# Moving whole-array blocks, reciprocals and graph weights within the attention loop of a two-layer graph kernel

## The chip, the cores and the metric

The kernel runs on one core of a Trainium2 chip. The metric is the device time of one execution in microseconds (us). The core has five engines with an instruction queue each: TensorE (PE in the profile, PEld for its weight loads), VectorE (DVE), ScalarE (ACT), GpSimd (POOL) and SyncE (SP, which here only issues DMAs). All arithmetic is float32.

## The reference

Input x has 16 batches of 1024 nodes with 256 channels; adj is a 1024 x 1024 matrix shared by the batches. Layer 0, cut to what matters here:

```python
c_adj = mean(fea, axis=1)                          # fea: x transposed to (B, 256, 1024)
diff  = c_adj[:, None, :] - c_adj[:, :, None]
A     = abs(abs(sigmoid(diff) - 0.5) - 0.5) * 2    # then made symmetric
g     = relu(einsum('bcn,bnm->bcm', fea, adj * A) * para)
q     = heads of g;  k, v = heads of x @ kv_w      # 4 heads of 64
out   = softmax(q @ k.T * scale) @ v
x     = layernorm(x + out)
```

Layer 1 is a graph convolution with the normalised adj, two linear layers with batch norms over all batches, a residual and a layernorm.

## The kernel before, in words

Layer 0 is one software-pipelined loop, layer 1 a plain sequence after it. The change touches the loop of layer 0 alone.

**Attention.** The scores are computed transposed (keys on the partitions) and the softmax is taken without a maximum: p = exp(scores), outputs and denominators are summed, and the outputs are divided at the end. The unit is (batch b, head pair pr, query half qh, key block m): 128 keys by 512 queries for two heads. `scores` (L768) runs its matmuls on quarters of the array, four side by side, into a PSUM tile ps (two buffers), and ScalarE takes the exponential into p (L773, four buffers). `outputs` (L789) multiplies p by v, also on quarters, accumulating over eight key blocks in two PSUM tiles po, and VectorE sums p into acc (L796 for the first two key blocks, L798 for the others). Eight units are a *group*. At its end ScalarE and VectorE bring po to oT (L802, L803).

**After a group.** `normalise` multiplies acc by ones (den, L813, quarters of the array, two PSUM tiles of the pool ps_t), ScalarE and VectorE add the two halves to drow (L818, L819), and SyncE writes drow to DRAM (den<-drow, L821) and gathers it back transposed as dcol (L824). VectorE takes the reciprocal r_all (L827). `residual` transposes oT (poT, L834, whole array), VectorE multiplies by r_all (o, L838), GpSimd adds to x (L843). With a batch's last group comes the layernorm: statistics on VectorE (L586, L587), the root on GpSimd (L577, L579), scaling on VectorE (L590), and a write of x to DRAM (L846).

**Preparing the next batch.** `prologue(b)` returns three lists. `first`: transposes of x (pxT, L671); the first of them also runs `begin`, which sums the rows of x (csum, L657), writes the negated means to DRAM element by element (c<-ncol, L662) and reads them back broadcast to all partitions (crow, L664). `side`: the weights, one Abs (L679) and one Tanh (L684, followed by VectorE's product with adj, L685) for each of eight node blocks, 16 entries in all; their eight buffers wg are shared by all batches. `steps`: four values (pv, L727, copied by VectorE, L731) and four keys (pk, L714, copied by ScalarE, L718), then 16 parts of the graph product pg (L697), of which every four end in qT on VectorE (L703) and ScalarE (L706). The steps use the whole array. Values and keys need xT; every four graph parts need all eight weights.

**The order.** Two units make a *burst*, so a batch has 16 bursts, numbered u = 0 to 15 here, and a group four. Iteration j of the loop issues the scores of burst j, the normalise that is due (two bursts after a group's end), and then, at the bursts that the table FULL names, a *whole-array block*: a due residual, four steps, and from u = 9 on some transposes of x. The outputs issued in iteration j are those of burst j - 1 (`back`). At u = 5 the x of two batches on is loaded (L633), into a buffer that the layernormed x of an earlier batch must have left.

TensorE's instructions keep this written order (`manual_schedule` names PE alone). On the other engines the planner of the language orders the instructions by when it believes that they can run, so a place in the source does not fix a place in those queues. Each engine then runs its queue in order, waiting on semaphores. All poT, pg, pv, pk, pxT and den tiles rotate through the two buffers of ps_t, so each must wait until the tile two before it has been read. SyncE's DMA issues are a queue in order too.

Of the kernel before, what the change touches and what calls it, by code (L numbers as in the profile page):

```python
# [515 lines left out]
def fast_path(  # L516
# [19 lines left out]
    nc = tc.nc  # L536
# [19 lines left out]
    def tile_t(name):  # L556
        return ps_t.tile([P, HALF], F32, tag="t", name=name)
# [23 lines left out]
    def layernorm(t, name):  # L581
        st = small.tile([P, NCH, 6], F32, tag="ln_st", name=f"st_{name}")
        mv = small.tile([P, NCH, 2], F32, tag="ln_mv", name=f"mv_{name}")
        rstd = small.tile([P, NCH], F32, tag="ln_rs", name=f"rs_{name}")
        for n in range(NCH):
            nc.vector.bn_stats(st[:, n, :], t[:, n, :])  # L586
            nc.vector.bn_aggr(mv[:, n, :], st[:, n, :])  # L587
        rsqrt(rstd, mv[:, :, 1], EPS)
        for n in range(NCH):
            nc.vector.tensor_scalar(  # L590
                t[:, n, :], t[:, n, :], mv[:, n, 0:1], rstd[:, n : n + 1], ALU.subtract, ALU.mult
            )
# [20 lines left out]
    with (  # L613
# [14 lines left out]
        r_all = l0c.tile([P, B * H, 4, 2], F32, name="r_all")  # L628
        st = {}

        def load_x(b):
            t = xp.tile([P, NCH, C], F32, tag="x", name=f"x_{b}")
            nc.sync.dma_start(t, x[b].rearrange("(n p) c -> p n c", p=P))  # L633
            st[b] = {"x": t}
# [125 lines left out]
        def scores(i):  # L760
            b, pr, qh, m = units[i]
            qT, kT = st[b]["qT"], st[b]["kT"]
            ps = tile_s(f"ps_{i}")
            for kh in range(2):
                for hd in range(2):
                    r = slice(hd * D, (hd + 1) * D)
                    ks = slice(m * P + kh * D, m * P + (kh + 1) * D)
                    nc.tensor.matmul(  # L768
                        ps[kh * D : (kh + 1) * D, hd * HALF : (hd + 1) * HALF], kT[r, pr, ks],
                        qT[r, pr, qh * HALF : (qh + 1) * HALF], start=True, stop=True,  # L770
                    )
            p = pp.tile([P, N], F32, tag="p", name=f"p_{i}")
            nc.scalar.activation(p, ps, AF.Exp)  # L773
            A[i] = p

        def outputs(i):
            b, pr, qh, m = units[i]
            s, p = st[b], A.pop(i)
            if m == 0:
                G[b, pr, qh] = {  # L780
                    "po": [tile_o(f"po_{i}_{kh}") for kh in range(2)],
                    "acc": accp.tile([P, N], F32, tag="acc", name=f"acc_{i}"),
                }
            g = G[b, pr, qh]
            for hd in range(2):
                h = 2 * pr + hd
                for kh in range(2):
                    r = slice(kh * D, (kh + 1) * D)
                    nc.tensor.matmul(  # L789
                        g["po"][kh][hd * D : (hd + 1) * D, :], s["v"][r, m, h * D : (h + 1) * D],  # L790
                        p[r, hd * HALF : (hd + 1) * HALF], start=(m == 0), stop=(m == NCH - 1),
                    )
            if m == 0:
                g["p0"] = p
            elif m == 1:
                nc.vector.tensor_add(g["acc"], g.pop("p0"), p)  # L796
            else:
                nc.vector.tensor_add(g["acc"], g["acc"], p)  # L798
            if m == NCH - 1:
                k = (b * PAIRS + pr) * 2 + qh  # L800
                g["oT"] = op.tile([P, HALF], F32, tag="oT", name=f"oT_{k}")
                nc.scalar.copy(g["oT"], g["po"][0])  # L802
                nc.vector.tensor_add(g["oT"], g["po"][1], g["oT"])  # L803

        def normalise(b, pr, qh):

            g = G[b, pr, qh]
            k = (b * PAIRS + pr) * 2 + qh
            den = [tile_t(f"den_{k}_{kh}") for kh in range(2)]
            for hd in range(2):  # L810
                for kh in range(2):
                    r = slice(kh * D, (kh + 1) * D)
                    nc.tensor.matmul(  # L813
                        den[kh][hd * D : (hd + 1) * D, :], ones[r, :],
                        g["acc"][r, hd * HALF : (hd + 1) * HALF], start=True, stop=True,
                    )
            row = rdp.tile([P, HALF], F32, tag="drow", name=f"drow_{k}")
            nc.scalar.copy(row, den[0])  # L818
            nc.vector.tensor_add(row, den[1], row)  # L819
            for hd in range(2):  # L820
                nc.sync.dma_start(den_d[k][hd : hd + 1, :], row[hd * D : hd * D + 1, :])  # L821
            col = small.tile([P, 4, 2], F32, tag="dcol", name=f"dcol_{k}")
            for hd in range(2):
                nc.sync.dma_start(  # L824
                    col[:, :, hd], den_d[k][hd : hd + 1, :].rearrange("o (n p) -> p (o n)", p=P)
                )
            nc.vector.reciprocal(r_all[:, k], col)  # L827

        def residual(b, pr, qh):
            g, s = G.pop((b, pr, qh)), st[b]  # L830
            k = (b * PAIRS + pr) * 2 + qh
            pt = tile_t(f"poT_{k}")
            for j in range(4):
                nc.tensor.transpose(  # L834
                    pt[:, j * P : (j + 1) * P], g["oT"][:, j * P : (j + 1) * P], ident
                )
            o = rdp.tile([P, 4, 2, D], F32, tag="o", name=f"o_{k}")
            nc.vector.tensor_mul(  # L838
                o, pt.rearrange("p (n h d) -> p n h d", h=2, d=D),
                r_all[:, k].unsqueeze(3).to_broadcast([P, 4, 2, D]),  # L840
            )
            xs = s["x"][:, 4 * qh : 4 * qh + 4, pr * P : (pr + 1) * P]
            nc.gpsimd.tensor_tensor(xs, xs, o.rearrange("p n h d -> p n (h d)"), ALU.add)  # L843
            if pr == PAIRS - 1 and qh == 1:
                layernorm(s["x"], f"l0_{b}")
                nc.gpsimd.dma_start(x1_d[b], s["x"])  # L846
                del st[b]

        def run(fs, k):
            for f, a in fs[:k]:  # L850
                f(*a)
            del fs[:k]
# [1 line left out]

        FULL = {1: 4, 4: 4, 6: 4, 9: 4, 11: 4, 14: 4}
        BURST = 2
        bursts = [range(i, i + BURST) for i in range(0, len(units), BURST)]
        PERB = PER // BURST  # L860
        with tc.manual_schedule(engines={mybir.EngineType.PE}):
            load_x(1)
            first, steps, side = prologue(0)
            run(first, 4)
            while steps:
                run(side, 4)
                run(steps, 2)
            next_first, next_steps, next_side = prologue(1)
            run(next_first, 4)
            full, quarter = {}, {}  # L870

            def back(j):

                for i in bursts[j]:
                    outputs(i)
                b, pr, qh, m = units[bursts[j][-1]]
                if m == NCH - 1:
                    quarter.setdefault(j + 2, []).append((normalise, (b, pr, qh)))
                    k = j + 4
                    while k % PERB not in FULL:  # L880
                        k += 1
                    full.setdefault(k, []).append((residual, (b, pr, qh)))

            for j in range(len(bursts)):
                b, u = j // PERB, j % PERB
                for i in bursts[j]:
                    scores(i)
                run(quarter.get(j, []), 9)
                if u == 0:
                    steps, side = next_steps, next_side  # L890
                    next_first, next_steps, next_side = [], [], []
                if u == 5 and b + 2 < B:
                    load_x(b + 2)
                    next_first, next_steps, next_side = prologue(b + 2)
                run(side, 3)
                if u in FULL:
                    run(full.get(j, []), 9)
                    run(steps, FULL[u])
                    if u >= 9:
                        run(next_first, 1 if u < 12 else 2)  # L900
                if j:
                    back(j - 1)
            j = len(bursts)
            back(j - 1)
            for k in range(j, j + 8):
                run(quarter.get(k, []), 9)
                run(full.get(k, []), 9)
# [278 lines left out]
```

## Time and profile before

The median of three runs is 3185.31 us (3184.79 to 3187.74); the profiled execution has a span of 3179.2 us.

| engine | busy us | share of the span |
|---|---|---|
| TensorE, matmuls | 2776.8 | 87% |
| TensorE, weight loads | 1213.2 | 38% |
| VectorE | 1416.8 | 45% |
| ScalarE | 1139.3 | 36% |
| GpSimd | 213.8 | 7% |

| group (one line, one engine) | count | busy us | mean ns |
|---|---|---|---|
| scores L768, TensorE | 4096 | 522.5 | 621 |
| outputs L789, TensorE | 4096 | 502.5 | 603 |
| graph product L697, TensorE | 1024 | 466.0 | 609 |
| exponentials L773, ScalarE | 512 | 499.1 | 1021 |
| accumulation L798, VectorE | 384 | 469.5 | 1223 |
| Abs L679 and Tanh L684, ScalarE | 256 | 271.2 | 1136 and 1043 |
| reciprocal L827, VectorE | 64 | 12.8 | 200 |

Matmuls are pipelined, so the mean of one is its latency, and busy us is the time in which at least one ran. The attention loop lasts until about 2070 us of the span; layer 1 follows. In the lines further down, the time in brackets is how long the engine stood idle before that instruction, and the name behind the arrow is what it was waiting for.

### The profile page before, as it was taken

Reading aid. Unit: us, or ns where it says so; the run is one execution under the profiler, and the core shown is the slowest. Engines: PE = TensorE matmul, PEld = TensorE weight load, DVE = VectorE, ACT = ScalarE, POOL = GpSimd, SP = SyncE. Lnnn points to the kernel's source line nnn. Section 1 sums busy time; section 2 is a strip of 40 time slices with the busy share of each in tenths; the row PEclk is TensorE's granted clock in tenths of the full one; section 3 lists DMA queues with packets and bytes.
Section 4 is the critical chain, followed back from the end, with each engine's and each line's share of the span. In section 5 each row is a group of like instructions: output and inputs, shape, how many; then the busy total and the mean of one; then the engine's idle time right before and its main releaser. Section 6 shows DMA issues by size and latency. Waiting matters only on the chain. (4 is left out here: it accounts for less than half of the span.)

```text
span 3179.2 us, 32796 instructions
## 1 busy us (share of the span) xinstructions
PE 2776.8 (87%) x13522; PEld 1213.2 (38%) x13522; DVE 1416.8 (45%) x2130; ACT 1139.3 (36%) x1313; POOL 213.8 (7%) x196
## 2 busy tenths in 40 slices
PE   6998898988988989889898899889999999999943
PEld 3433333333333333333333333364444444444432
DVE  3554554654545545455465454641111111233365
ACT  3454352552534535434255253400011111133284
POOL 0000001000000001000100000100000000000032
PEclk9999999998999999999999999969999999999955
DMA  4000101101011010010100101102212221144255
GB/s 126 8 19 16 34 1 34 28 7 34 1 34 33 2 34 15 20 34 1 34 28 8 34 1 38 31 27 93 96 76 80 79 80 66 53 172 159 106 185 199
DMA packets 122062, 169.00 MB, mean 53 GB/s; under 512 B 86704, under 2 KB 103600, under 8 KB 111664
## 3 DMA queue, kind: packets, MB, share of 16 engines
q1 hardware_dynamic: 112720, 99.70, 10.4%
q0 software_dynamic: 9184, 67.12, 5.3%
q8 instruction: 108, 1.77, 0.3%
q14 instruction: 50, 0.41, 0.0%
HBM read 99.36 MB, written 67.44 MB: 52 GB/s over the span
## 5 line engine op out<-in xcount | busy, mean ns | idle before, releaser
L768 PE MATMUL ps<-qT,kT 64*64 64x512 f32 x4096 | 522.5, 621 | 148.7 <-ACT p L773 148.7
L773 ACT ACTIVATE p<-ps 128x1024 f32<-128x1024 f32 x512 | 499.1, 1021 | 291.3 <-PE ps L768 290.6
L798 DVE TENSOR_TENSOR acc<-acc,p 128x1024 f32<-128x1024 f32 x384 | 469.5, 1223 | 251.7 <-ACT p L773 235.2
L789 PE MATMUL po<-p,v 64*64 64x512 f32 x4096 | 502.5, 603 | 4.9 <-DVE oT L803 4.9
L697 PE MATMUL pg<-wg,x 128*128 128x512 f32 x1024 | 466.0, 609 | 20.7 <-DVE drow L819 17.1
L998 PE MATMUL pagg<-ahT,x1l 128*128 128x512 f32 x1024 | 444.0, 593 | 0.0
L768 PEld LDWEIGHTS ps<-qT,kT 64*64 64x64 f32 x4096 | 155.5, 138 | 461.1 <-issue 233.3
L1017 ACT ACTIVATE hw<-ph,col_b 128x1024 f32<-128x1024 f32 x64 | 71.3, 1114 | 651.3 <-PE ph L1013 651.3
L697 PEld LDWEIGHTS pg<-wg,x 128*128 128x128 f32 x1024 | 193.8, 194 | 272.8 <-issue 247.4
L998 PEld LDWEIGHTS pagg<-ahT,x1l 128*128 128x128 f32 x1024 | 194.2, 190 | 241.1 <-issue 241.1
L789 PEld LDWEIGHTS po<-p,v 64*64 64x64 f32 x4096 | 152.0, 136 | 296.7 <-issue 286.1
L843 POOL TENSOR_TENSOR x<-x,o 128x512 f32<-128x512 f32 x64 | 109.0, 1704 | 1833.7 <-DVE o L838 1833.7
L706 ACT ACTIVATE qT<-qT 128x512 f32<-128x512 f32 x64 | 40.1, 626 | 532.5 <-DVE qT L703 532.5
L1077 PE MATMUL po<-hl,w2T 128*128 128x512 f32 x512 | 222.4, 597 | 6.9 <-ACT hl L1068 6.9
L1013 PE MATMUL ph<-agg,w1T 128*128 128x512 f32 x512 | 222.2, 592 | 0.0
L1002 DVE COPY agg<-pagg 128x1024 f32<-128x1024 f32 x32 | 39.2, 1224 | 377.8 <-PE pagg L998 377.8
L727 PE MATMUL pv<-kvw_s,xT 128*128 128x256 f32 x512 | 147.7, 439 | 57.5 <-DVE v L731 28.9
L685 DVE SCALAR_TENSOR_TENSOR wg<-wg,adj_s 128x1024 f32<-128x1024 f32 x128 | 153.3, 1219 | 36.7 <-ACT wg L684 36.7
L1019 DVE BATCH_NORM_STATS2 bn_st<-hw 128x6 f32<-128x512 f32 x128 | 82.3, 685 | 152.4 <-ACT hw L1017 152.4
L1077 PEld LDWEIGHTS po<-hl,w2T 128*128 128x128 f32 x512 | 98.1, 192 | 131.1 <-issue 122.4
L727 PEld LDWEIGHTS pv<-kvw_s,xT 128*128 128x128 f32 x512 | 108.5, 220 | 100.8 <-DVE v L731 42.1
L1013 PEld LDWEIGHTS ph<-agg,w1T 128*128 128x128 f32 x512 | 97.3, 190 | 122.5 <-issue 122.5
(87 smaller groups left out, 2011.4 us busy)
## 6 DMA issues: line engine op xcount, KB each, us to landing
h<-hw POOLq DMA_DIRECT2D x16, 2048.0 KB, 6.5
hl<-h SPq DMA_DIRECT2D x16, 2048.0 KB
x<-in_x_dram SPq DMA_DIRECT2D x16, 1024.0 KB
x<-x POOLq DMA_DIRECT2D x16, 1024.0 KB, 4.2
x1l<-x SPq DMA_DIRECT2D x16, 1024.0 KB
xf<-x SPq DMA_DIRECT2D x16, 1024.0 KB
out_dram<-xf POOLq DMA_DIRECT2D x16, 1024.0 KB, 5.2
crow<-c SPq DMA_DIRECT2D x16, 512.0 KB
```

Of the source, the lines that this page charges most:

```text
L685: nc.vector.scalar_tensor_tensor(w, w, 1.0, adj_s[:, n, :], op0=ALU.subtract, op1=ALU.mult)
L697: nc.tensor.matmul(ps, xt[:, n, c * P : (c + 1) * P], s["wg", n][:, hs], start=(n == 0), stop=(n == NCH - 1),)
L727: nc.tensor.matmul(pt[:, j * C : (j + 1) * C], s["xT"][:, c, n * P : (n + 1) * P], kvw_s[:, c, C : 2 * C], start=(c == 0), stop=(c == CC - 1),
L768: nc.tensor.matmul(ps[kh * D : (kh + 1) * D, hd * HALF : (hd + 1) * HALF], kT[r, pr, ks], qT[r, pr, qh * HALF : (qh + 1) * HALF], start=Tr ...
L773: nc.scalar.activation(p, ps, AF.Exp)
L789: nc.tensor.matmul(g["po"][kh][hd * D : (hd + 1) * D, :], s["v"][r, m, h * D : (h + 1) * D], p[r, hd * HALF : (hd + 1) * HALF], start=(m = ...
L798: nc.vector.tensor_add(g["acc"], g["acc"], p)
L843: nc.gpsimd.tensor_tensor(xs, xs, o.rearrange("p n h d -> p n (h d)"), ALU.add)
L998: nc.tensor.matmul(ps[:, hs], xt[:, m, c * P : (c + 1) * P], ahT[:, m, hs], start=(m == 0), stop=(m == NCH - 1),)
L1013: nc.tensor.matmul(ps[:, hs], w1T[:, c, k * P : (k + 1) * P], t[:, c, hs], start=(c == 0), stop=(c == CC - 1),)
L1019: nc.vector.bn_stats(bn1_st[:, k, 2 * b + half, :], ht[:, k, half * HALF : (half + 1) * HALF])
L1077: nc.tensor.matmul(ps[:, hs], w2T[:, k, c * P : (c + 1) * P], ht[:, k, hs], start=(k == 0), stop=(k == HC - 1),)
```

## The change

Four things are done together.

- The table FULL moves the six whole-array blocks from bursts 1, 4, 6, 9, 11, 14 to bursts 0, 4, 6, 8, 10, 12, and within an iteration the outputs (`back`) are now issued ahead of the block. At bursts 0, 4, 8 and 12 those outputs end a group, so the block stands between a group's last outputs and the next group's work, while oT is brought out of PSUM. The transposes of x move to bursts 10 and 12.
- The reciprocal is issued in `residual`, where its result is used, in place of `normalise`, where its operand has just been asked for from DRAM.
- A residual falls due five bursts after its group's last burst in place of four.
- The 16 entries of the weights are issued over ten bursts: two each at bursts 13, 14 and 15 of the batch before, and the other ten at bursts 0 to 5, one where a block stands and two elsewhere. Before, they were issued three at a time from burst 0 on. For batch 1 the first six are issued ahead of the loop.

```diff
         def normalise(b, pr, qh):
...
-            nc.vector.reciprocal(r_all[:, k], col)
+            g["col"] = col
 
         def residual(b, pr, qh):
             g, s = G.pop((b, pr, qh)), st[b]
             k = (b * PAIRS + pr) * 2 + qh
+            nc.vector.reciprocal(r_all[:, k], g["col"])
...
-        FULL = {1: 4, 4: 4, 6: 4, 9: 4, 11: 4, 14: 4}
+        FULL = {0: 4, 4: 4, 6: 4, 8: 4, 10: 4, 12: 4}
...
             run(next_first, 4)
+            run(next_side, 6)
...
-                    k = j + 4
+                    k = j + 5
                     while k % PERB not in FULL:
                         k += 1
...
-                run(side, 3)
+                if j:
+                    back(j - 1)
                 if u in FULL:
                     run(full.get(j, []), 9)
                     run(steps, FULL[u])
-                    if u >= 9:
-                        run(next_first, 1 if u < 12 else 2)
-                if j:
-                    back(j - 1)
+                    if u >= 10:
+                        run(next_first, 2)
+                if u > 12:
+                    run(next_side, 2)
+                else:
+                    run(side, 1 if u in FULL else 2)
```

## The prediction

> **What bounds the kernel now.** I read the page first, then who waits for whom on TensorE between 179 and 2029 us (the attention part), then the engines in order of time through one batch.
>
> ```profile
> PE 2776.8 (87%) x13522; PEld 1213.2 (38%) x13522; DVE 1416.8 (45%) x2130; ACT 1139.3 (36%) x1313; POOL 213.8 (7%) x196
> ...
> PE   6998898988988989889898899889999999999943
> ...
> PEclk9999999998999999999999999969999999999955
> ```
> TensorE is the bound. It is nearly full in the graph convolution (slices 27 to 37), but loses a tenth to a fifth in the attention slices, and those are what the change touches. Nothing after about 2070 us should move.
>
> ```profile
> PE ps L768 <- ACT p L773: 146.6, 51, 10.2
> PE pv L727 <- DVE v L731: 25.4, 14, 1.8
> PE poT L834 <- ACT drow L818: 24.2, 29, 0.8
> PE pv L727 <- DVE drow L819: 19.7, 14, 1.8
> PE pg L697 <- DVE drow L819: 16.0, 14, 1.1
> ```
> Columns: us in all, times, longest. So 60 us (24.2 + 19.7 + 16.0) come from whole-array blocks that start right after a denominator (den) and find both ps_t buffers taken. The large item, ps behind the exponentials p, is in time order on TensorE:
>
> ```profile
> 763.55 1.90 PE L789 MATMUL po<-p,v 64*64 64x512 f32 x16
> 775.68 3.69 PE L768 MATMUL ps<-qT,kT 64*64 64x512 f32 x16 [10.23 <-ACT p L773]
> 779.14 3.01 PE L789 MATMUL po<-p,v 64*64 64x512 f32 x16
> ...
> 785.56 0.66 PE L834 MATMUL poT<-ident,oT 128*128 128x128 f32 x4 [0.83 <-ACT drow L818]
> 787.35 8.83 PE L697 MATMUL pg<-wg,x 128*128 128x512 f32 x16 [1.14 <-DVE drow L819]
> ```
> TensorE stands 10.23 us at burst 8, then runs its next 16 matmuls in 3.69 instead of 1.90 us. The cause is on VectorE, ScalarE and the DMA queue:
>
> ```profile
> 758.23 2.29 DVE L657 TENSOR_REDUCE csum<-x 128x8 f32<-128x2048 f32 x1 [6.63 <-DMA x<-in_x_dram]
> 760.43 0.68 DVE L819 TENSOR_TENSOR drow<-den,drow 128x512 f32<-128x512 f32 x1
> ...
> 773.29 0.20 DVE L827 RECIPROCAL r_all<-dcol 128x8 f32<-128x8 f32 x1 [9.57 <-DMA dcol<-den]
> 773.41 0.64 DVE L703 SCALAR_TENSOR_TENSOR qT<-pg,para_s 128x512 f32<-128x512 f32 x1
> ```
> ```profile
> 774.08 0.63 ACT L706 ACTIVATE qT<-qT 128x512 f32<-128x512 f32 x1 [19.86 <-DVE qT L703]
> ```
> ```profile
> 753.02 0.37 SPq L633 DMA_DIRECT2D x<-in_x_dram  x1
> 761.14 0.54 SPq L821 DMA_DIRECT2D den<-drow  x2
> 761.77 0.38 SPq L662 DMA_DIRECT2D c<-ncol  x1
> 762.29 1.03 SPq L824 DMA_DIRECT2D dcol<-den  x2
> ```
> The row sum csum holds VectorE until x has landed, drow queues behind it, the gather dcol is issued behind the scattered write c, and the reciprocal waits 9.57 us. Behind it stands qT, behind that ScalarE's qT, then the exponentials of burst 7, then TensorE.
>
> **What the Trainium skill says.** "TensorE: Matmul & The Clock Gate", section "Architectural detail", has ScalarE and VectorE as strict FIFOs; the 19.86 us of ScalarE agree. The same page, "What's actually happening", has TensorE's clock halved after about 3.4 us of idleness; 3.69 against 1.90 us agree. "DMA: Bandwidth & Descriptors", "Rules for kernel authors", makes a strided last dimension one descriptor per element, and "Queues, rings and completion order" has each ring taken in order. Here c (4 KB) needs 10.5 us until crow, which waits for it, is issued (772.28), and dcol behind it needs 11.0 (762.29 to 773.29); at burst 9, without c, dcol lands 2.7 us after its issue (788.48 to the reciprocal at 791.21). Agreed.
>
> **One batch in numbers.** Burst 8 comes round every 129.7 us (256.47 to 1812.59 in 12 steps). Idle TensorE per batch: burst 8, mean 8.3 (13 stalls of 6.0 to 10.2); den before a block at bursts 1 and 9, 4.1; values at burst 4, 1.8; weights at burst 15, 2.8 (1.83 + 0.77 + 0.2); pxT, 0.35; 17.4 in all. Undisturbed work: 16 bursts x 3.43 (726.86 to 730.29), 6 blocks of about 7.1, den 4 x 0.87, transposes 8 x 0.5: 105.7. The remaining 6.6 us per batch is half clock.
>
> **Part by part.** I take the instruction order of the changed program as built, since only TensorE's order is written by hand, and lay the durations above along it.
>
> *Reciprocals.* Written later, but the planner still puts each on VectorE one accumulation after its drow, as it can run as soon as dcol is there. So this line alone buys little. What does change at burst 5: drow now stands ahead of csum, and dcol ahead of c on the queue. From the end of the GpSimd residual addition P (burst 4): layernorm ends P+7.1 (739.2 to 746.3); x is there 11.9 later (746.3 to 758.23), P+19.0; csum, ccol, ncol to P+21.6; accumulation, reciprocal, accumulation, qT: P+24.8 if dcol has landed; ScalarE's qT and one exponential: P+26.5; scores P+26.7. TensorE would be ready at P+24.4 (values resume P+2.2; second half of block 3.5; then S, den, O, S, O, graph block, S, O, with 0.4 lost at den). Stall 2.3 instead of 8.3. Dcol: its den write queues behind the load of x (issued P+13.8), so it lands between P+18 (2.7 after issue) and about P+22; the reciprocal's turn is P+22.8. Bounds: 1 if x comes sooner, 6 if the load or c slows dcol. I take 2.3: 6.0 x 13 = **78 us saved**.
>
> *Blocks at 0, 4, 6, 8, 10, 12.* None shares a burst with a den (1, 5, 9, 13) now: the 4.1 us go, in all 26.5 + 19.7 + 17.1 = **63 us saved**. No matmul is added. The evacuation oT that blocks behind group ends would hide cost TensorE only one wait of 4.9 in the whole trace: nothing. New small waits: values at burst 0 behind two batch-norm statistics, 0.5; burst 4, 0.2 more, as an accumulation goes ahead of o; den at burst 5 on the v copy behind the layernorm, 0.4; a second pxT wait at burst 10, 0.35; den at 13 behind xT, 0.3. 1.75 x 15 = **26 us lost**.
>
> *Weights over ten bursts.* As built they are not spread: the weight buffers come free with the last graph block (burst 12 now), and ScalarE gets all 16 Abs and Tanh after oT there, before the exponentials of burst 14, with only burst 13's two, one qT and one drow among them. In before, at burst 15, 14 such instructions took 13.5 us (690.60 to 704.09), 0.96 each; the 20 here take 19.2, from 0.7 after the block's start, plus the exponential: scores of burst 15 may go 21 us after the block's start. TensorE has until then: block 6.9, two pxT with their wait 1.8, S 1.7, den with wait 1.2, O, S, O 5.2: 16.8. Stall 4.3 instead of 2.8: 1.5 x 15 = **22 us lost**. Bounds 3.5 to 6.
>
> *Half clock.* No row shows it for this order. Bounds: none, or 7 per batch as now. After a 6 us stall, scores and outputs lost 1.8 + 1.1; the 1.82 us wait for values lost nothing (1.99 for the next part). I take about 2.9 for burst 15's stall and 0.9 for the rest: 3.8 against 6.6, 2.8 x 13 = **36 us saved**.
>
> Sum: 78 + 63 - 26 - 22 + 36 = 129; 3185 - 129 = **3056 us**.
>
> **Rivals.**
> (a) The stall at burst 8 stays. For it: the reciprocal is still early on VectorE, csum still waits for x, and den now queues behind the load. Against: dcol no longer follows c. Then the 78 and the half clock go: 63 - 26 - 22 = 15, about 3170 us; with dcol a little slower yet, 3150 to 3185.
> (b) Slower: as (a), and the clump of weights stalls 7 or more with its own half clock (another 3 + 3 per batch, 90 us): about 3250. For it: the clump is now contiguous before burst 14. Against: the count above gives 4.3.
> (c) Faster yet: short waits leave the clock whole and dcol arrives early; half clock near zero (50 more) and burst 8 at 1 us (17 more): about 2990.
>
> **How the numbers follow.** Forecast 0.72, (a) 0.12, (b) 0.05, (c) 0.11. The forecast's own spread: half clock 0 to 7 gives -50 to +42, burst 8 from 1 to 6 gives -17 to +48, burst 15 -12 to +25; together about 3005 to 3120. Leaving half of (c), all of (b) and most of (a) outside gives 3005 to 3125. Faster 0.93 (part of (a) is near no change), same 0.02, slower 0.05.
>
> **What would show it.** The wait of ps for p should fall from 147 to about 90 us, in two groups: near 2.3 at burst 8 and near 4.3 at burst 15. Waits of poT, pv and pg for drow should vanish. VectorE's wait for dcol, 204.5 us in all, should fall by more than half, and csum's wait for x stay near 6 to 8 each. The period of a batch should be near 120 us. I am wrong if the reciprocal still waits about 10 us at burst 6, if the load of x shifts, or if the weights stall TensorE more than 6 us.

## The result, and the profile after

The changed kernel takes 2991.39 us (median of 4 runs, 2989.65 to 2992.18) against 3186.52 us for the kernel before on the same chip. The ratio is 0.9381, with a 95% interval of 0.9362 to 0.9401. So it is faster, by more than forecast: 3056 us was forecast, and the time lies 14 us below the range. The profiled execution has a span of 2990.3 us.

The page of the changed kernel, first TensorE's busy time, then its busy tenths and its granted clock in 40 slices:

```profile
PE 2736.4 (92%) x13522; PEld 1202.2 (40%) x13522; DVE 1418.0 (47%) x2130; ACT 1138.6 (38%) x1313; POOL 185.7 (6%) x196
...
PE   6999999999999999999999999799999999999842
...
PEclk9999999999999999999999999699999999999955
```

The number of instructions is the same on every engine, and the busy time of VectorE and ScalarE has not moved by more than 1.2 us. All attention slices of TensorE between the first and the last now show a 9 where 8 and 9 alternated: the gain is mostly waiting time that went. GpSimd is busy 28 us less, which matters further down.

TensorE's waits in the attention part of the changed kernel (179 to 1900 us): us in all, times, longest.

```profile
PE ps L768 <- ACT p L773: 69.6, 20, 4.5
PE pv L727 <- DVE v L731: 12.7, 14, 0.9
PE pxT L671 <- DVE qT L703: 9.0, 26, 0.3
```

The scores' wait for exponentials fell from 146.6 to 69.6 us, values' wait for their copies from 25.4 to 12.7, and the three waits for drow are gone. The 26 waits for pxT are the 0.35 at bursts 10 and 12, two in most batches.

One batch of the changed kernel in order of time, all engines, around burst 8 (burst 4 at the top, SPq is the DMA queue):

```profile
571.22 1.99 PE L727 MATMUL pv<-kvw_s,xT 128*128 128x256 f32 x8 [0.91 <-DVE v L731]
...
580.66 0.37 SPq L633 DMA_DIRECT2D x<-in_x_dram  x1
...
586.09 0.93 SPq L824 DMA_DIRECT2D dcol<-den  x2
586.15 2.29 DVE L657 TENSOR_REDUCE csum<-x 128x8 f32<-128x2048 f32 x1 [5.92 <-DMA x<-in_x_dram]
...
588.75 0.36 SPq L662 DMA_DIRECT2D c<-ncol  x1
...
589.76 0.20 DVE L832 RECIPROCAL r_all<-dcol 128x8 f32<-128x8 f32 x1
...
591.09 0.68 DVE L703 SCALAR_TENSOR_TENSOR qT<-pg,para_s 128x512 f32<-128x512 f32 x1
...
593.42 1.98 PE L768 MATMUL ps<-qT,kT 64*64 64x512 f32 x16
```

The gather dcol is now issued 2.66 us ahead of the scattered write c. The reciprocal, before which VectorE stood idle for 9.57 us in the batch shown of before, has no bracket: it starts without a wait that the view shows. The scores of burst 8, which followed a hole of 10.23 us, have none either.

What is left is at burst 15. TensorE of the changed kernel, and then ScalarE:

```profile
649.25 3.69 PE L768 MATMUL ps<-qT,kT 64*64 64x512 f32 x16 [4.46 <-ACT p L773]
652.72 2.54 PE L789 MATMUL po<-p,v 64*64 64x512 f32 x16
```
```profile
644.22 2.18 ACT L679 ACTIVATE wg<-crow,ccol 128x1024 f32<-128x1024 f32 x2
646.30 2.00 ACT L684 ACTIVATE wg<-wg 128x1024 f32<-128x1024 f32 x2
648.19 1.92 ACT L773 ACTIVATE p<-ps 128x1024 f32<-128x1024 f32 x2
```

The exponentials of burst 14 stand behind the last of 16 Abs and Tanh, which follow each other from 629.48 on with only the two exponentials of burst 13, one qT and one drow among them. The two groups of matmuls behind the hole take 3.69 and 2.54 instead of 1.90 us.

A batch now takes 115.5 us (burst 15 from 300.93 to 1686.67 in 12 steps) instead of 129.7.

### The profile page after: what moved, and what is told of

Its sections match the earlier page's. It is cut to its first block, busy times and chain, and to the rows that moved or that the text cites. A ratio compares the mean times of both kernels' runs of the same rounds, so it can differ in the third digit from the quotient of the medians.

```text
span 2990.3 us, 32734 instructions
## 1 busy us (share of the span) xinstructions
PE 2736.4 (92%) x13522; PEld 1202.2 (40%) x13522; DVE 1418.0 (47%) x2130; ACT 1138.6 (38%) x1313; POOL 185.7 (6%) x196
## 5 line engine op out<-in xcount | busy, mean ns | idle before, releaser
L768 PE MATMUL ps<-qT,kT 64*64 64x512 f32 x4096 | 519.1, 619 | 69.6 <-ACT p L773 69.6
L697 PE MATMUL pg<-wg,x 128*128 128x512 f32 x1024 | 454.4, 597 | 4.3 <-ACT kT L718 4.3
L789 PEld LDWEIGHTS po<-p,v 64*64 64x64 f32 x4096 | 166.3, 137 | 292.8 <-issue 289.6
L844 POOL TENSOR_TENSOR x<-x,o 128x512 f32<-128x512 f32 x64 | 81.1, 1267 | 1670.3 <-DVE o L839 1670.3
L727 PE MATMUL pv<-kvw_s,xT 128*128 128x256 f32 x512 | 128.0, 394 | 26.8 <-DVE v L731 16.1
L679 ACT ACTIVATE wg<-crow,ccol 128x1024 f32<-128x1024 f32 x128 | 140.8, 1137 | 17.2 <-PE pg L697 11.9
```

The source lines that it names most:

```text
L679: nc.scalar.activation(w, s["crow"], AF.Abs, bias=s["ccol"][:, n : n + 1])
L697: nc.tensor.matmul(ps, xt[:, n, c * P : (c + 1) * P], s["wg", n][:, hs], start=(n == 0), stop=(n == NCH - 1),)
L727: nc.tensor.matmul(pt[:, j * C : (j + 1) * C], s["xT"][:, c, n * P : (n + 1) * P], kvw_s[:, c, C : 2 * C], start=(c == 0), stop=(c == CC - 1),
L768: nc.tensor.matmul(ps[kh * D : (kh + 1) * D, hd * HALF : (hd + 1) * HALF], kT[r, pr, ks], qT[r, pr, qh * HALF : (qh + 1) * HALF], start=Tr ...
L789: nc.tensor.matmul(g["po"][kh][hd * D : (hd + 1) * D, :], s["v"][r, m, h * D : (h + 1) * D], p[r, hd * HALF : (hd + 1) * HALF], start=(m = ...
```

## The experiments

Ratios are against the kernel before on the same chip; three chips were used. The kernel before took 3185.2 us on that of the first four experiments below, 3208.83 on that of the means on another queue and of the first three experiments with an order written by hand, and 3188.2 on that of the other three. So ratios are compared, not times.

**Reciprocal alone.** The kernel before, with the one line moved.

```diff
-            nc.vector.reciprocal(r_all[:, k], col)
+            g["col"] = col
 ...
 def residual(b, pr, qh):
+            nc.vector.reciprocal(r_all[:, k], g["col"])
```

> The kernel before with one part of the change: the reciprocal issued in residual. As built, the instruction order of VectorE, ScalarE and the DMA queue is that of before, line for line. Theory A (the order that the planner gives decides, the place in the source does not): no change, 3180 to 3190 us, burst 8 still stalls 6 to 10 us. Rival B (the reciprocal's place frees VectorE): 3050 to 3110 us, burst 8 stalls under 3 us.

Measured: 3186.98 us, ratio 1.0006 (0.9994 to 1.0018). The waits are those of before (ps for p 146.8). The planner orders VectorE here, and moving this line in the source did nothing.

**Blocks alone.** The changed kernel, with the reciprocal and the weights issued as before.

```diff
...
-            run(next_side, 6)
...
-                if u > 12:
-                    run(next_side, 2)
-                else:
-                    run(side, 1 if u in FULL else 2)
+                run(side, 3)
```

> The changed kernel with the reciprocal back in normalise and the weights issued three a burst as before; what is left is the table of blocks, the outputs ahead of the block, and the residual's fifth burst. Theory A: the whole gain is here, 2985 to 3000 us. Rival B: the reciprocal and the weights carry a good part of it, 3040 us or more.

Measured: 2992.84 us, ratio 0.9389 (0.937 to 0.9407). The whole gain is in the table, the outputs ahead of the block and the residual's fifth burst. Spreading the weights in the source gained nothing: in the changed kernel all 16 still stand together behind burst 12's block.

**Outputs ahead of the block alone.** The kernel before with its old table.

```diff
+                if j:
+                    back(j - 1)
                 if u in FULL:
...
-                if j:
-                    back(j - 1)
```

> The kernel before with only the outputs issued ahead of the whole-array block; its table 1, 4, 6, 9, 11, 14 stays. As built, drow then stands ahead of csum on VectorE and dcol ahead of c on the queue. Theory A: burst 8 falls from 8.3 us to 0 to 2.5 (13 times), den has outputs of 1.7 us between it and the block, so the waits for drow fall from 60 us to under 10, and ScalarE's clump of weights now stalls TensorE about 4.5 us a batch: near 3000 us, 2980 to 3040. Rival C (the table's positions are what counts): 3110 us or more.

Measured: 2979.18 us, ratio 0.9347 (0.9328 to 0.9366): this alone gives all of it, and a little more than the whole change. The waits of this kernel on TensorE:

```profile
PE ps L768 <- ACT p L773: 61.1, 35, 3.1
PE pv L727 <- DVE v L731: 12.8, 14, 0.9
...
PE pv L727 <- DVE drow L819: 5.2, 12, 0.9
```

The hole at burst 8 falls to 0.6 us in the mean, in 5 of 13 batches. With the outputs ahead, drow has 1.7 us of matmuls more to be computed in, so even blocks that share a burst with a denominator hardly wait: of the 60 us of drow waits, 5.2 are left before pv and 4.4 before pg, without a new table. The holes in front of the scores that the weights leave are 0.56 and 3.11 us per batch, together 3.7 in place of 4.46.

**The table alone.** The changed kernel with the outputs behind the block again, except at u = 0.

```diff
-                if j:
+                if j and u == 0:
                     back(j - 1)
                 if u in FULL:
...
+                if j and u:
+                    back(j - 1)
```

> The changed kernel with the outputs back behind the block (except at burst 0, where values would overwrite a v still in use). As built, csum stands ahead of drow and c ahead of dcol again, as in before. Theory A: the waits for drow go (4.1 us a batch), burst 8 stalls 6 to 10 us as before, the clump of weights 4 to 5: 3110 to 3170 us. Rival C: 3000 to 3040 us.

Measured: 3091.46 us, ratio 0.9703 (0.9682 to 0.9724), better than expected. The drow waits are gone, but the hole at burst 8 stays (8.3 us in the mean). Burst 15, where the expectation put 4 to 5 us, has a hole of only 1.52 here; waits for oT of 14 us in all, which the whole change does not have, take back a part. DMA queue of this kernel, then TensorE:

```profile
729.95 0.53 SPq L821 DMA_DIRECT2D den<-drow  x2
730.58 0.38 SPq L662 DMA_DIRECT2D c<-ncol  x1
731.09 1.04 SPq L824 DMA_DIRECT2D dcol<-den  x2
```
```profile
732.11 1.90 PE L789 MATMUL po<-p,v 64*64 64x512 f32 x16
743.98 3.69 PE L768 MATMUL ps<-qT,kT 64*64 64x512 f32 x16 [9.97 <-ACT p L773]
```

Here csum still stands ahead of drow and c ahead of dcol. So it is the outputs ahead of the block that turn both orders round.

**The means on another queue.** Is it the queue that makes dcol late, or the DMA engines? The kernel before, with c and crow issued by GpSimd.

```diff
-                nc.sync.dma_start(c_d[b].rearrange("o (n p) -> p (o n)", p=P), ncol)
+                nc.gpsimd.dma_start(c_d[b].rearrange("o (n p) -> p (o n)", p=P), ncol)
...
-                nc.sync.dma_start(s["crow"], c_d[b][0].partition_broadcast(P))
+                nc.gpsimd.dma_start(s["crow"], c_d[b][0].partition_broadcast(P))
```

> The kernel before with the means' write c and read crow issued by GpSimd, so that dcol no longer stands behind c in SyncE's queue; csum still stands ahead of drow on VectorE. Theory A (c ahead of dcol is what makes the reciprocal late): dcol lands about 2.7 us after its issue, the stall at burst 8 falls from 8.3 to about 2.3 us in 13 batches with its half clock: 3070 to 3110 us. Rival D (what counts is csum ahead of drow, or the 16 DMA engines are shared so that c delays dcol from any queue): burst 8 stalls 5 us or more, 3140 us or more.

Measured: 3195.63 us, ratio 0.996 (0.9946 to 0.9974), so next to nothing; the hole at burst 8 has a mean of 8.7 us. SyncE's queue of this kernel, then GpSimd's, then VectorE:

```profile
769.13 0.53 SPq L821 DMA_DIRECT2D den<-drow  x2
770.28 0.96 SPq L824 DMA_DIRECT2D dcol<-den  x2
```
```profile
769.55 0.93 POOL L662 DMA_DIRECT2D c<-ncol  x1 [14.46 <-DVE ncol L661]
780.19 0.57 POOL L664 DMA_DIRECT2D crow<-c  x1 [9.71 <-DMA c<-ncol]
```
```profile
781.15 0.20 DVE L827 RECIPROCAL r_all<-dcol 128x8 f32<-128x8 f32 x1 [9.44 <-DMA dcol<-den]
```

The gather, with c on another queue, still needs 10.87 us (770.28 to 781.15); c started 0.73 us earlier. The Trainium skill says in "DMA: Bandwidth & Descriptors", section "Issuing engines are not separate DMA queues", that DMAs of all engines end on the same 16 DMA engines. The run agrees, since the other queue did not bring the gather near the 2.7 us that it needs without c. My reading in the prediction, that the gather waits because it is issued behind c on one queue, was wrong in that detail. What is left as the reason is which starts first; the next run tests it.

**The means after the gather.** The counterpart: the kernel before, in which ncol is made to depend on the reciprocal of the group under way (its value times zero is added), so that c cannot start before dcol has landed. csum stays ahead of drow.

```diff
+                if b >= 3:
+                    late = small.tile([P, NCH], F32, tag="late", name=f"late_{b}")
+                    nc.vector.scalar_tensor_tensor(
+                        late, r_all[:, (b - 2) * H].rearrange("p n h -> p (n h)"), 0.0, csum,
+                        op0=ALU.mult, op1=ALU.add,
+                    )
+                    csum = late
                 nc.vector.tensor_scalar(ncol, csum, -1.0 / C, None, ALU.mult)
```

> The kernel before, with the negated means ncol of a batch (from batch 3 on) computed from csum + 0 x r_all of the group whose denominators are on their way, so that the scattered write c can only be issued once dcol has landed and its reciprocal is done. csum still stands ahead of drow on VectorE; one VectorE operation of about 0.16 us per batch is added; nothing of the result changes. Theory (c, once started, holds the DMA engines, and dcol waits for them): dcol lands about 3 us after its issue in place of 11, the stall of TensorE at burst 8 falls from 8.3 to about 2, the wait of ps for p from 147 to about 60-80 us, and the ratio is near 0.965 (0.955 to 0.975). Rival (the cause is that csum, waiting for x, holds drow back; c only adds a little): stall of 5 or more, ratio above 0.985.

Measured: 3061.02 us, ratio 0.9604 (0.9588 to 0.962), within the theory's range. DMA queue of this kernel, then VectorE, in one batch:

```profile
725.19 0.53 SPq L828 DMA_DIRECT2D den<-drow  x2
726.34 0.93 SPq L831 DMA_DIRECT2D dcol<-den  x2
729.76 0.36 SPq L669 DMA_DIRECT2D c<-ncol  x1
740.22 0.34 SPq L671 DMA_DIRECT2D crow<-c  x1
```
```profile
722.28 2.29 DVE L657 TENSOR_REDUCE csum<-x 128x8 f32<-128x2048 f32 x1 [6.71 <-DMA x<-in_x_dram]
...
729.13 0.20 DVE L834 RECIPROCAL r_all<-dcol 128x8 f32<-128x8 f32 x1 [1.43 <-DMA dcol<-den]
```

The gather lands 2.79 us after its issue in place of 11.0, and c takes its 10.5 us where nobody waits for it. The hole of burst 8 falls to a mean of 0.8 us (12 of 13 batches still have one, of 0.2 to 2.5), although csum is still ahead of drow. So the order of c and dcol in time is the cause of nearly all of that hole, and the place of csum of some tenths at most.

**A slower residual addition.** In the changed kernel the last GpSimd addition of a batch takes 1.27 us; in the one before it took 2.18. Here a second, unused addition of 128 x 384 is put ahead of it.

```diff
+            if pr == PAIRS - 1 and qh == 1:
+                twice = small.tile([P, 3, P], F32, tag="twice", name=f"twice_{k}")
+                nc.gpsimd.tensor_tensor(
+                    twice, xs[:, 0:3], o.rearrange("p n h d -> p n (h d)")[:, 0:3], ALU.add
+                )
             nc.gpsimd.tensor_tensor(xs, xs, o.rearrange("p n h d -> p n (h d)"), ALU.add)
```

> The changed kernel with one more GpSimd addition (128 x 384, result unused) ahead of the last residual addition of each batch, so that this step takes about 2.2 us as in the kernel before, in place of 1.27. Theory (the prediction's two sizes at bursts 4 and 8 were too large because this addition is faster and the layernorm behind it ends earlier): the wait of pv for v at burst 4 goes from 0.9 to about 1.8 and the mean stall at burst 8 from 0.4 to about 1.2, so about 1.7 us x 13 = 22 us more than the changed kernel plus some half clock: ratio 0.945 to 0.953 against 0.938. Rival (the chain has slack from elsewhere, such as the earlier arrival of x): pv waits 1.8, burst 8 stays near 0.4, ratio 0.940 to 0.943.

Measured: 3021.05 us, ratio 0.9478 (0.9463 to 0.9494). The ratio is in the theory's interval, but the theory fell in half: the wait for values rose to 2.0 as expected (27.8 us in 14), while the hole at burst 8 did not grow; 2 of 13 batches have one (0.54 and 1.44). TensorE of this kernel at burst 4:

```profile
576.81 2.72 PE L727 MATMUL pv<-kvw_s,xT 128*128 128x256 f32 x8 [1.98 <-DVE v L731]
579.32 2.89 PE L714 MATMUL pk<-xT,kvw_s 128*128 128x512 f32 x4
```

The addition delays TensorE, through the values, by as much as it delays the chain that ends at burst 8, so the two still meet. The rest of the lost time is clock: behind the 1.98 us shown, the next two groups take 2.72 and 2.89 in place of 1.99 and 1.88. That happens in 9 of 14 batches and costs 1.74 us each time; the next section says why not in the others. Together a batch is 1.4 us longer than that of the changed kernel, about 0.8 by idle time and 0.7 by clock.

**ScalarE's order written by hand.** The changed kernel, where the planner no longer bunches the weights.

```diff
-        with tc.manual_schedule(engines={mybir.EngineType.PE}):
+        with tc.manual_schedule(engines={mybir.EngineType.PE, mybir.EngineType.Activation}):
```

> The changed kernel with ScalarE also kept in the written order, so that the weights are really spread over ten bursts. Theory A (the planner's clump causes the 4.5 us stall at burst 15 and most of the half clock left): the stall goes, period from 115.5 to about 109 us, 2880 to 2930 us. Rival E (a written order on ScalarE brings new waits, for instance exponentials behind a Tanh or behind qT): 2960 us or more.

Measured: 2948.9 us, ratio 0.9198 (0.9182 to 0.9213), against 0.9381 for the change and between the two expectations. The wait of ps for p falls to 10.0 us. Waits for VectorE to read a ps_t buffer come in its place (pv for v 32.6, pk for o 14.4), together 47 us.

**Outputs ahead and ScalarE by hand.** The same with the outputs-first version, in which three weights are issued per burst.

```diff
-        with tc.manual_schedule(engines={mybir.EngineType.PE}):
+        with tc.manual_schedule(engines={mybir.EngineType.PE, mybir.EngineType.Activation}):
...
+                if j:
+                    back(j - 1)
                 if u in FULL:
...
-                if j:
-                    back(j - 1)
```

> The kernel before with only the outputs ahead of the block, and ScalarE in the written order (weights three a burst). Theory A: the stalls of 0.6 and 3.1 us around bursts 15 and 0 go: 2890 to 2940 us. Rival E: three weights a burst make ScalarE (1.94 + 3 x 0.96 = 4.8 us) longer than TensorE's burst of 3.43 and bring waits of their own: 2960 us or more.

Measured: 3035.07 us, ratio 0.9467 (0.9452 to 0.9483): slower than with the planner's order (0.9347). Rival E holds. pk waits 68.7 us for o, and in the trace o stands on VectorE behind products of the weights with adj, which wait for Tanh. That three weights in a burst are too many for a hand-written ScalarE is read from this and not shown, since this version differs from that of the preceding experiment in its table too.

**VectorE's order by hand as well.**

```diff
-        with tc.manual_schedule(engines={mybir.EngineType.PE}):
+        with tc.manual_schedule(engines={mybir.EngineType.PE, mybir.EngineType.Activation, mybir.EngineType.DVE}):
```

> The changed kernel with ScalarE and VectorE both in the written order, so that the reciprocal really stands at its use. VectorE's wait for dcol (72 us in all in the changed kernel) should be near zero. Theory A: the reciprocals' waits are hidden already, so this gives at most 10 us over the run with ScalarE alone, and VectorE's written order (layernorm and csum in one piece) may cost more: 2880 to 3000 us. Rival F (the reciprocal's place matters once it is real): 30 us or more below the run with ScalarE alone.

Measured: 3064.47 us, ratio 0.9556 (0.954 to 0.9572), a miss. Now the reciprocal really runs at its use, and pk waits 69.7 us for v and 38.4 for o, up to 5.0 at once. With ScalarE by hand, the planner's VectorE order is better than that of the source (0.9198 against 0.9556).

**Weights inside the block of burst 12.** ScalarE by hand, with six weights between the graph parts of that block and two each at bursts 13 to 15 and 1 to 3.

```diff
-        with tc.manual_schedule(engines={mybir.EngineType.PE}):
+        with tc.manual_schedule(engines={mybir.EngineType.PE, mybir.EngineType.Activation}):
...
-                    run(steps, FULL[u])
+                    for i in range(FULL[u]):
+                        run(steps, 1)
+                        if u == 12 and i < 3:
+                            run(next_side, 2)
...
-                    run(side, 1 if u in FULL else 2)
+                    run(side, 2 if b == 0 or u in (1, 2, 3) else 0)
```

> The version with ScalarE's order as written, with the weights issued so that they can start when their buffers come free: six between the graph parts of burst 12's block, two each at bursts 13 to 15 and 1 to 3, none at 0, 4 and 5. Theory (what is left there is ScalarE's copies of values and keys held up by weights in the same bursts): waits of pv for v and pk for o fall from 47 to about 20 us, ratio about 0.910 against 0.920. Rival (the weights in burst 12 delay the last qT and the exponentials as much as they free elsewhere): 0.920 or more.

Measured: 2919.82 us, ratio 0.916 (0.9145 to 0.9176), between the two expectations. pv for v and pk for o fall from 47.0 to 28.4 us, not to 20. It is the fastest version, 8.4% below the kernel before.

## Why the prediction was wrong in its size

The direction and the bound were right, and so was the mechanism in the main: the hole at burst 8 shrank because dcol went ahead of c. (It is the time at which the two start that counts, not the queue, and the outputs ahead of the block turned them round; the prediction did not say which part of the change would.) Two terms of the sum were mis-sized: the hole at burst 8 and the small waits. Point by point, for one batch:

| step of the prediction | predicted | measured |
|---|---|---|
| hole at burst 8 | 2.3 | 0.4 (2.07, 1.42, 0.65 and 0.81 in 4 of 13 batches, else none) |
| drow waits ahead of blocks | gone | gone |
| values at burst 4 | 1.8 + 0.2 | 0.91 |
| waits at bursts 0, 5 and 13 | 0.5, 0.4, 0.3 | none |
| pxT at bursts 10 and 12 | 0.35 more | 0.35 more |
| hole at burst 15 | 4.3 | 4.46 |
| half clock | 3.8 | 3.3 as the remainder (115.5 less 105.7 of work and 6.5 idle), 2.4 by the record of the clock |

**The hole at burst 8** (forecast 78 us saved, about 103 had: 8.3 less 0.4, times 13). The chain was right but for one link: "x is there 11.9 later (746.3 to 758.23)". That is one batch of the kernel before, and of its 13 batches the slowest: from the layernorm's end to csum it takes 9.76 to 11.93 us, 10.0 in the median, and 11.9 was taken for all. In the changed kernel it is 9.75 to 12.38, and the hole follows it to about 0.01 us: 12.38, 11.72, 11.11 and 10.95 give 2.07, 1.42, 0.81 and 0.65, so hole = delay less 10.30, and the nine batches below 10.30 have none. The spread comes in three of these four from when the load can be issued (4.6 to 6.9 us after the layernorm's end), which waits until the write of the old x has left the buffer. Even the slow batch would have had 1.6 and not 2.3: the chain behind csum was 0.45 shorter than predicted, and TensorE came to the scores some 0.25 later. My lower bound, 1 "if x comes sooner", had no reason to stop above zero.

The changed kernel at the end of that chain, in one of the four batches with a hole, all engines:

```profile
697.64 0.37 SPq L633 DMA_DIRECT2D x<-in_x_dram  x1
...
702.81 2.29 DVE L657 TENSOR_REDUCE csum<-x 128x8 f32<-128x2048 f32 x1 [7.54 <-DMA x<-in_x_dram]
...
707.75 0.68 DVE L703 SCALAR_TENSOR_TENSOR qT<-pg,para_s 128x512 f32<-128x512 f32 x1
...
710.06 2.00 PE L768 MATMUL ps<-qT,kT 64*64 64x512 f32 x16 [1.42 <-ACT p L773]
```

From csum to the scores 7.25 us pass, against 7.7 in the prediction.

**The small waits** (forecast 26 us lost; 0.91 won at burst 4 less 0.35 lost at pxT, times 14, is 8 saved). I wrote "burst 4, 0.2 more, as an accumulation goes ahead of o", and let the GpSimd addition behind o keep the 2.18 us that it had. GpSimd and VectorE of the kernel before show why it had them:

```profile
737.02 2.18 POOL L843 TENSOR_TENSOR x<-x,o 128x512 f32<-128x512 f32 x1 [18.81 <-DVE o L838]
```
```profile
736.25 0.69 DVE L838 TENSOR_TENSOR o<-poT,r_all 128x512 f32<-128x512 f32 x1 [1.24 <-PE poT L834]
736.86 1.22 DVE L796 TENSOR_TENSOR acc<-p,p 128x1024 f32<-128x1024 f32 x1
```

An accumulation with both inputs in SBUF runs beside it until 738.08, and the addition takes 0.9 longer than the 1.27 us that it takes alone. This is no chance of one batch: of the 64 additions of before, the 31 beside an accumulation take 2.17 to 2.19, and the other 33 take 1.25 to 1.27. In the changed kernel the accumulation goes ahead of o, and all 64 take 1.25 to 1.28 us. So the same reordering that I charged with 0.2 takes 0.9 off. The Trainium skill has it in "SBUF — State Buffer", section "SBUF: two separate sides": a VectorE operation with two SBUF inputs and a GpSimd operation hold one port pair in turn, each for its whole length. The traces agree, with 2.18 beside one and 1.27 without. In the version with the slowed addition the wait is back at 2.0, the forecast's figure. The waits at bursts 0, 5 and 13 I counted from queue positions, and in the trace each copy is done by the time that TensorE needs it, at burst 5 to within 0.05 us (v done at 576.65, den starts at 576.70).

**Half clock** came out near its size, in part by luck. Behind burst 15's hole the next two groups lose a mean of 2.3 us in 13 batches (1.4 to 3.0 each), not 2.9, which I had from one batch; and the loss of 1.8 + 1.1 that I put behind "a 6 us stall" stands behind the hole of 10.23. The 105.7 us of work is also uncertain: its own items add up to 105.0, and by the traces it is nearer 107. Counted from the record of the granted clock, as half the time that TensorE was busy at half clock, the loss is 5.0 us per batch before and 2.4 after.

That record also shows what a wait costs. In the 13 traces of this case the granted clock changes only at moments that lie whole multiples of 3.41 us apart. Four stretches of this grid in the changed kernel, around the hole at burst 15 (from 644.79 to 649.25); the columns are the stretch, its length, how long TensorE was busy, its matmuls, the granted clock, and the share and GB/s of the DMA engines:

```profile
643.77:647.18 3.41, 1.03 (x12) 1.00 0.11 2
647.18:650.59 3.41, 1.33 (x8) 0.50 0.05 0
650.59:654.01 3.42, 3.42 (x20) 0.50 0.02 5
654.01:657.42 3.41, 3.41 (x36) 1.00 0.00 0
```

A stretch with much idle time is followed by one at half clock, a full one by full clock. From 180 to 1850 us of all 13 traces, 241 stretches at full clock were followed by one at half: in each, TensorE was idle for 1.80 us or more. In the 5732 that were followed by full clock it was idle for at most 2.02. So what counts is the idle time inside one stretch, with the border between 1.8 and 2.0 us. The waits for values of 0.91 and 1.82 us, 28 in the two kernels, lost nothing. Those of 1.98, in the kernel with the slowed addition, lost time in 9 of 14, and two waits of 1.82 and 0.77 close together, at burst 15 of before, in 4 of 14. A hole of 2.15 in the outputs-first version was divided by the grid and lost nothing, while one of 2.07 in the changed kernel lost 1.8. The prediction took 3.4 us of idleness from the Trainium skill, "TensorE: Matmul & The Clock Gate", section "What's actually happening"; a loss needs less than that here, and the measurement decides.

**The sum again**: 103 + 63 + 8 - 23 (1.66 at burst 15, 14 times) + 43 (3.3 of half clock, times 13) = 194, and 3185 - 194 = 2991 us, as measured. It closes because the 3.3 is a remainder: by the record of the clock, half clock accounts for 34 of these 43, and the other 9 were not traced. Of the 65 us missing from the forecast's sum, 25 are the hole at burst 8, 34 the small waits and 7 the half clock, less 1 at burst 15.

Rival (c) named 2990 us and is nearest, but its number is luck: only its small hole at burst 8 was as it said, half clock did not go near zero, and it kept the 26 us of small waits. Rivals (a) and (b) fell, since dcol did go ahead of c, and the weights' hole was 4.46, not 7 or more.

The credit to the table was too high: the prediction counted the 63 us for moving blocks off the bursts with a denominator. The table alone does remove these waits, but so do the outputs ahead of the block, with the old table, all but 10 us of them.

What stays open: why the write of the old x, and so the load, is up to 2.3 us later in some batches; no run varied it. And why the outputs-first version is a little faster than the whole change (0.9347 against 0.9381) is only read from its trace and was not tested: per batch it is idle for 6.2 us in place of 6.6, and half clock costs 1.1 in place of 2.4, for behind its holes of 0.56 and 3.11 no stretch at half clock is longer than 3.41 us, where in the changed kernel 9 of 15 last 6.83.

## What to carry to other kernels

Take a duration that sets a chain from all its occurrences and give its spread: one batch read as typical was the slowest of 13. When a reordering puts two operations side by side or apart, look whether one of them has two durations in the trace, and which goes with which neighbour. A remainder of a sum closes it by construction; find it in the trace by itself. Where a planner orders the queues, change what it sees (here the outputs ahead of the block turned two orders round), since moving a line in the source can leave the program as it was.

## What the hardware showed beyond that

- A scattered write of 4 KB (c, one element each) keeps crow, which waits for it, from being issued for 8.5 to 11.9 us (13 batches of before, median 10.5). A gather that starts up to 0.8 us behind it needs 8.7 to 11.8 us, from its own queue or from another; ahead of it, the same gather lands in 2.7 to 3.4 in the run with the means after it.
- A GpSimd addition of 128 x 512 takes 1.27 us, and 2.18 beside a VectorE accumulation with two inputs in SBUF.
- TensorE's granted clock changes on a grid of 3.41 us. After a stretch of the grid with 1.79 us of idle time or less it stayed whole, after one with 2.03 or more it was halved for at least the next stretch, and between them both were seen.
